# Attention's loads on GpSimd's queue, a bias made from its predecessor, and a fifth tile for the float16 probabilities

## The chip, the cores and the metric

The kernel runs on one core of a Trainium2 chip. The metric is the device time of one execution in microseconds (us), the median of several runs. The profile shows one further execution. Engines are named as in the profile: PE (TensorE matmuls), PEld (its weight loads), DVE (VectorE), ACT (ScalarE), POOL (GpSimd) and SP (SyncE); "SPq" is SP's queue, in which it issues DMAs in order.

## What is computed

A layer norm of x (1024 x 512) feeds two branches: grouped-query attention with 32 heads, 8 key/value heads and a linear position bias (ALiBi), and a feed-forward block with 4-bit weights. The result is x + attention * silu(ffn). The attention part of the reference, cut to what matters:

```python
q = _rmsnorm(q, q_norm_w); k = _rmsnorm(k, k_norm_w)
scores = jnp.einsum('bkgqd,bksd->bkgqs', qg, k) / math.sqrt(HD)
slopes = jnp.asarray(_alibi_slopes(H)).reshape(HKV, G)   # start * start**i, start = 2**(-1/4)
rel = pos[None, :] - pos[:, None]
bias = jnp.where(rel > 0, NEG_INF, slopes[:, :, None, None] * rel)
attn = jax.nn.softmax(scores + bias[None], axis=-1)
out = jnp.einsum('bkgqs,bksd->bkgqd', attn, v)
...
return out @ Wo.T
```

## The kernel before

The order of instructions on every engine is the order in which the program is written; there is no scheduler. The stages are: layer norm and the gate and up matmuls (to about 130 us), the down matmul (to about 215 us), twelve projections of keys, values and queries (to about 470 us), and the attention with its output projection (to the end). The last two projections share their time with the first eight steps of the attention.

Products keep near float32 precision: an operand is split into a high and a low part, and `mm3` (L108 to L110) adds three products. So keys (`kT`), values (`vT`), queries (`qT`) and probabilities are pairs of float16 tiles.

The projections write keys, values and queries to scratch in DRAM (`kd`, `vd`, `qd`). The attention loads them again: `load_keys` and `load_values` once a group of four heads (512 KB each), `load_queries` once a block of 256 query rows (512 KB), `load_wo` four times a group (256 KB each, output weights), and `gate_load` for the last four blocks (two of 512 KB each). All of these are issued by SP before the change.

A group has four blocks of 256 queries (qb = 0 to 3). Because of the causal mask, a block qb needs (qb + 1) x 256 keys at most. Groups 1 to 6 take the blocks in the order 2, 3, 0, 1; group 0 takes 3, 2, 1, 0; group 7 takes 2, 3, 1, 0. A block has four heads with two tiles of 128 queries each: eight steps, 256 steps in all. A tile's width is 128 to 1024 keys, so qb = 3 is called the wide block.

What happens to one tile, with the step at which it is issued (`step`):

- step n: `scores` on PE (tile s); PE waits where the two s tiles are still in use.
- step n + 1: `exponentials`. DVE adds the bias (`trel`, scaled for the head by `cs`) and finds the minimum (L799); ACT makes the exponential and its sum (L800), into `pf`.
- step n + 3: `split_hi`. ACT writes the high half of the scaled probabilities into a tile p16 (L810). The pool has `P16_BUFS` of these tiles, so it waits until the transpose of the tile so many places before has landed.
- step n + 4: `split_lo`. DVE writes the low half (L819), and SP issues the DMA that transposes the tile into `pT` (L820).
- step n + 9 (`AV_LAG`): `values` on PE multiplies pT with vT.

After that come `heads_hi` (ACT, L847), `heads_lo` (DVE, L853), `out_proj` (PE) and `accumulate` (DVE), one block later. `split_wo` splits the output weights: ACT writes woh (L769), POOL subtracts to get wol (L770). Raw weights `wor` have two buffers, which wol frees. `load_wo` stands 10 steps ahead of the projection it serves, `split_wo` 6 steps.

POOL also normalizes keys and queries in the projections (`newton` and `normalize`, tile f, L582 to L597), before DVE's `halves` (L608 to L610). That work for the last projection is spread over the attention, two tiles at a time. The bias of a group, `trel`, is made by POOL in `relative` (L775) from a fixed table of key minus query positions, `nrel` (L719 to L722), which is in SBUF throughout; `rc` is the reciprocal of the scale `cs`. `trel` has two buffers. A table or trel takes 4 KB of each partition, as does a p16 tile.

Of the kernel before, what the change touches and what calls it, by code (L numbers as in the profile page):

```python
# [10 lines left out]
F32 = mybir.dt.float32  # L11
# [5 lines left out]
ALU = mybir.AluOpType  # L17
# [4 lines left out]
P = 128  # L22
S = 1024
# [3 lines left out]
NH = 4  # L27
HD = 128
# [7 lines left out]
NQT = QB // P  # L36
# [22 lines left out]
GATE_SUMS = [27, 28, 30, 31]  # L59
GATE_STEP = 2  # L60
PF_BUFS = 5
P16_BUFS = 4

_START = 2 ** (-(2 ** (-(math.log2(H) - 3))))
SLOPES = np.array([_START * _START**i for i in range(H)], dtype=np.float32)
# [5 lines left out]
def attention_gated_by_ffn_kernel(ctx, tc, x, gu_w, gu_z, gu_s, dn_w, dn_z, dn_s, wq, wkv, wo, qnw, knw, out):  # L71
    nc = tc.nc
    ve, se, ge, te, sp = nc.vector, nc.scalar, nc.gpsimd, nc.tensor, nc.sync
# [46 lines left out]
    rc = const.tile([P, 1], F32, name="rc")  # L120
# [3 lines left out]
    kd = [dram.tile([P, 2, NT, 2 * HD], F16, name=f"kd{i}") for i in range(HKV // 2)]  # L124
    vd = [dram.tile([P, NT, 2 * HD], F16, name=f"vd{g}") for g in range(HKV)]
    qd = [dram.tile([NT, P, 2 * NH * HD], F16, name=f"qd{g}") for g in range(HKV)]
    ald = [dram.tile([1, 2 * HD], F32, name=f"ald{i}") for i in range(HKV // 2)]
    gd = dram.tile([NT, P, DM], F32, name="gd")
# [323 lines left out]
    def finish_step():  # L452

        for f in finishing.pop(clock[0], ()):
            f()
        clock[0] += 1
# [172 lines left out]
    def prepare(k, t):  # L629

        if k < len(projections):
            p = projections[k]
            if t == -1:
                p.squares()
            elif t == 1:
                p.norms()
            elif t == 2:
                p.scale()
            elif t == 6:
                p.factors()  # L640
            if 2 <= t < 2 + p.n:
                p.split_head(t - 2)
            elif p.kind == "kv" and 4 <= t < 6:
                p.split_values(t - 4)
# [31 lines left out]
    for it in range(NI):  # L676
        for tb in range(2):
# [14 lines left out]
            for i in range(4):  # L692
                c = slice(i * P, i * P + P)
# [23 lines left out]
    vp16 = left.enter_context(tc.tile_pool(name="values", bufs=1))  # L717
    fq = ctx.enter_context(tc.tile_pool(name="finish", bufs=2, side="right"))
    ap1 = ctx.enter_context(tc.tile_pool(name="attn1", bufs=2, side="right"))  # L719
    nrel = ap1.tile([P, S], F32, name="nrel", bufs=1)  # L720
    ge.iota(nrel, pattern=[[-1, S]], base=S - P, channel_multiplier=1, allow_small_or_imprecise_dtypes=True)
    ge.affine_select(nrel, nrel, pattern=[[-1, S]], compare_op=ALU.is_ge, fill=1e20, base=S - P, channel_multiplier=1)  # L722

    def queue_half(p, half):

        last = p is projections[-1]

        def due(steps, i, f):
            t = half * HT + i
            c = TILES - early + BS * (NB * (1 + t // 2) + FINISH_BLOCK) + 4 * (t % 2) if last else clock[0] + i  # L730
            finishing.setdefault(c + steps, []).append(f)

        due(0, 0, lambda: p.inverse(half))
        for i in range(3):
            due((i + 1) // 2, 0, lambda i=i: p.newton(half, i == 2))
        for i in range(HT):
            t = half * HT + i
            due(4, i, lambda t=t: p.halves(t))
            due(2, i, lambda t=t: p.normalize(t))
# [4 lines left out]
    kT, vT, qT, woh, wol = {}, {}, {}, {}, {}  # L744
    trel, pT, oT, wor = {}, {}, {}, {}

    def load_keys(g):
        kT[g] = ap1.tile([P, NT, 2, P], F16, tag="kT", name=f"kT{g}")
        sp.dma_start(kT[g].rearrange("p t a k -> p t (a k)"), kd[g // 2][:, g % 2])

    def load_values(g):
        vT[g] = ap1.tile([P, NT, 2, HD], F16, tag="vT", name=f"vT{g}")
        sp.dma_start(vT[g].rearrange("p t a d -> p t (a d)"), vd[g])

    def load_queries(g, qb):
        qT[g, qb] = ap1.tile([P, NQT, 2, NH, P], F16, tag="qT", name=f"qT{g}_{qb}")
        sp.dma_start(
            qT[g, qb].rearrange("p t a g q -> p t (a g q)"), qd[g][qb * NQT : (qb + 1) * NQT].rearrange("t p c -> p t c")
        )

    def load_wo(g, i):
        wor[g, i] = late[0].tile([P, DM], F32, tag="wor", name=f"wor{g}_{i}", bufs=2)
        sp.dma_start(wor[g, i], wo[(g * NH + i) * HD : (g * NH + i + 1) * HD, :])

    def split_wo(g, i):
        woh[g, i] = late[0].tile([P, DM], F32R, tag="woh", name=f"woh{g}_{i}", bufs=5)
# [4 lines left out]

    def relative(g):

        trel[g] = ap1.tile([P, S], F32, tag="trel", name=f"trel{g}")
        ge.tensor_scalar(trel[g], nrel, rc, float(SLOPES[g * NH + NH - 1]), ALU.mult, ALU.mult)  # L775

    s_ps, pf, rows16, p16, av_ps, op_ps = {}, {}, {}, {}, {}, {}

# [24 lines left out]
    def split_hi(u, qt):  # L803
# [4 lines left out]
        nk = pf[u, qt].shape[1]  # L808
        p16[u, qt] = ap1.tile([P, NT, 2, P], F16, tag="p16", name=f"p16_{u}_{qt}", bufs=P16_BUFS)[:, :nk]
        se.activation(p16[u, qt][:, :, 0, :], pf[u, qt], AF.Copy, scale=scale[:, qt : qt + 1])  # L810
# [56 lines left out]
    def gate_load(b):  # L867
        g, qb = blocks[b]
        gx = fq.tile([P, 2, NQT, DM], F32, tag="f", name=f"gx{qb}", bufs=3)
        t0 = qb * NQT  # L870
        sp.dma_start(gx[:, 0], gd[t0 : t0 + NQT].rearrange("t p c -> p t c"))
        sp.dma_start(gx[:, 1], x[t0 * P : (t0 + NQT) * P, :].rearrange("(t p) c -> p t c", p=P))
        gates[b] = gx

    def gate_partial(b, i):
# [30 lines left out]
    def step(n):  # L906
        nonlocal last_ps
        if n < nn:
            u, qt = order[n]
            g, qb, hh = units[u]  # L910
            b = u // NH
            if qt == 0 and hh == 1 and b + 1 < nb:
                load_queries(*blocks[b + 1])
            if qt == 0 and hh == 3 and g + 1 < HKV:
                if b % NB == KEYS_BLOCK:
                    relative(g + 1)
                    load_keys(g + 1)
                elif b % NB == VALUES_BLOCK:
                    load_values(g + 1)
            scores(u, qt)  # L920
# [34 lines left out]
        if r == 2 and b in GATE_LOADS:  # L955
            gate_load(nb - NB + GATE_LOADS.index(b))
        if b in GATE_SUMS and 0 <= r - GATE_STEP < NQT:
            gate_partial(nb - NB + GATE_SUMS.index(b), r - GATE_STEP)
        for lead, act in ((WO_SPLIT, split_wo), (WO_LOAD, load_wo)):
            w, r = divmod(m + lead, NB * BS)  # L960
            if 0 <= w < HKV and r in range(0, 2 * NH, 2):
                act(w, r // 2)

    last_ps = None
    early = 0
    for k, p in enumerate(projections):
        if k == len(projections) - 3:
            load_keys(0)
            load_values(0)
            load_queries(*blocks[0])  # L970
            relative(0)
        for t in range(NT):
            prepare(k + 1, t)
            if t == NT - 1:
                prepare(k + 2, -1)
            if k + 2 < len(projections) and t < KT:
                projections[k + 2].load(t)
            if t == HT:
                p.undo()
            p.tile(t)  # L980
            finish_step()
            if t % HT == HT - 1:
                queue_half(p, t // HT)
            if k >= len(projections) - 2 and t % 2 == 0:
                step(early)
                early += 1
# [46 lines left out]
```

## Time and profile before

| | |
|---|---|
| Time before | 1084.39 us median of 3 runs (1084.32 to 1085.37) |
| The profiled execution | 1091.69 us, span 1089.9 us |
| Mean granted PE clock | 0.984 |
| DMA issues of the attention's loads | 32 qT, 32 wor, 8 kT, 8 vT, 8 gx, all on SP |
| Transposes of p (pT<-p) | 256, median 4.0 us from issue to landing |

How to read it: the span is that of the profiled execution from its first to its last instruction. A stage's line lists for each engine the time in which it was busy and its instructions. A line of waits says who waited for whom, for how many us in total, how often, and the longest. In a timeline, a line has its start, its duration, engine, line of the program, operation, what is written from what, and in brackets the idle time before it with what ended it. An idle engine costs nothing unless the end of the program waits for it.

### The profile page before, as it was taken

What the parts mean: (1) busy time and instruction counts of PE and PEld (TensorE: products, weight loads), DVE (VectorE), ACT (ScalarE), POOL (GpSimd) and SP (SyncE); (2) the same over time, 40 slices, a digit from 0 to 9 for tenths busy, and PEclk for the clock granted to TensorE, in tenths of its full rate; (3) what the DMA queues carried; (4) which work ended last, traced back from release to release, by engine and by line L of the source; (5) the groups of instructions that cost most, each with busy time, mean ns of one, the idle gap of its engine ahead of it and who ended that gap; (6) DMA issues with size and microseconds to landing.
All of it is one profiled execution on the core that took longest, in us unless ns stands there. A gap on an engine that the chain in (4) does not pass through costs nothing.

```text
span 1089.9 us, 18604 instructions
## 1 busy us (share of the span) xinstructions
PE 1026.4 (94%) x5912; PEld 622.4 (57%) x5912; DVE 887.6 (81%) x1746; ACT 792.0 (73%) x2123; POOL 415.9 (38%) x551
## 2 busy tenths in 40 slices
PE   7899899999999898997999999999998999999986
PEld 4444378744444343445666666666665566666664
DVE  7888987448878888886898896998897878969974
ACT  5777633568786786787887796896886878868961
POOL 1588663137877878641105013023040030132222
PEclk8999999999999999998999999999999999999998
DMA  6123155237989999999989999998998999999993
GB/s 198 47 98 125 60 160 141 89 106 164 226 219 208 241 200 259 228 189 212 213 187 199 197 206 187 202 210 183 198 203 182 196 205 176 203 222 206 235 203 88
DMA packets 445888, 198.11 MB, mean 182 GB/s; under 512 B 394402, under 2 KB 403934, under 8 KB 445790
## 3 DMA queue, kind: packets, MB, share of 16 engines
q1 hardware_dynamic: 445790, 196.93, 82.6%
q8 instruction: 46, 0.75, 0.3%
q14 instruction: 52, 0.43, 0.2%
HBM read 71.03 MB, written 29.36 MB: 92 GB/s over the span
## 4 chain that ended last, share of the span: by engine, by line
PE 59%; DMA 13%; DVE 11%; ACT 8%; issue 5%; POOL 3%; SPq 1%; DVEq 0%; ACTq 0%; POOLq 0%
DMA pT<-p 12%; PE gu_ps L252 6%; PE av L108 4%; PE s L108 4%; PE s L109 4%; PE s L110 4%; PE av L109 4%; PE av L110 4%; PE ps_q L109 3%; PE ps_q L110 3%; PE op L110 3%; PE op L108 3%; PE ps_q L108 3%; PE op L109 3%; PE dn_ps L110 2%
## 5 line engine op out<-in xcount | busy, mean ns | idle before, releaser
L819 DVE SCALAR_TENSOR_TENSOR p<-pf,row,p 128x1024 f16<-128x1024 f32 (+7 forms) x256 | 216.6, 846 | 76.9 <-ACT p L810 74.8
L810 ACT ACTIVATE p<-pf,row 128x1024 f16<-128x1024 f32 (+7 forms) x256 | 197.0, 770 | 73.7 <-DMA pT<-p 70.2
L800 ACT ACTIVATE pf<-pf,row 128x1024 f32<-128x1024 f32 (+7 forms) x256 | 197.2, 770 | 38.5 <-DVE row L799 36.7
L770 POOL TENSOR_TENSOR wol<-wor,woh 128x512 fp32r<-128x512 f32 x32 | 59.8, 1870 | 429.5 <-ACT woh L769 373.6
L799 DVE CUSTOM_DVE_ANT_0 pf<-s,trel,cs 128x1024 f32<-128x1024 f32 (+7 forms) x256 | 207.5, 810 | 4.1 <-PE s L110 4.0
L108 PE MATMUL av<-pT,vT 128*128 128x256 f16 (+1 forms) x640 | 171.7, 268 | 25.2 <-DMA pT<-p 24.8
L109 PE MATMUL av<-pT,vT 128*128 128x256 f16 (+1 forms) x640 | 169.2, 264 | 0.0
L110 PE MATMUL av<-pT,vT 128*128 128x256 f16 (+1 forms) x640 | 169.0, 264 | 0.0
L108 PE MATMUL s<-kT,qT 128*128 128x512 f16 (+3 forms) x384 | 125.5, 327 | 6.6 <-DVE row L799 6.2
L109 PE MATMUL s<-kT,qT 128*128 128x512 f16 (+3 forms) x384 | 125.4, 327 | 0.0
L110 PE MATMUL s<-kT,qT 128*128 128x512 f16 (+3 forms) x384 | 123.8, 327 | 0.0
L108 PEld LDWEIGHTS <-vT 128*128 128x128 f16 x640 | 62.5, 98 | 106.9 <-issue 84.8
L108 PE MATMUL op<-woh,oh 128*128 128x512 f32 x248 | 121.7, 491 | 0.0
L109 PE MATMUL ps_q<-wl_q,xth 128*128 128x512 f16 x256 | 98.2, 383 | 6.7 <-DVE wl_q L528 6.7
L110 PE MATMUL op<-woh,ol 128*128 128x512 f32 x248 | 99.1, 400 | 0.0
L110 PE MATMUL ps_q<-wh_q,xtl 128*128 128x512 f16 x256 | 98.3, 384 | 0.0
L109 PE MATMUL op<-wol,oh 128*128 128x512 f32 x248 | 97.9, 395 | 0.4 <-POOL wol L770 0.4
L108 PE MATMUL ps_q<-wh_q,xth 128*128 128x512 f16 x256 | 98.2, 384 | 0.0
L847 ACT ACTIVATE oh<-av,rv 128x256 fp32r<-128x256 f32 x128 | 58.9, 460 | 24.9 <-PE av L110 24.4
L853 DVE SCALAR_TENSOR_TENSOR ol<-av,rv,oh 128x256 fp32r<-128x256 f32 x128 | 61.3, 479 | 13.6 <-ACT oh L847 13.5
L597 POOL TENSOR_TENSOR f_q<-f_q,inv_q 128x512 f32<-128x512 f32 x64 | 71.2, 1132 | 1.4
L109 PEld LDWEIGHTS <-vT 128*128 128x128 f16 x640 | 63.7, 100 | 12.2 <-issue 2.7
(179 smaller groups left out, 2315.1 us busy)
## 6 DMA issues: line engine op xcount, KB each, us to landing
qd<-tr_q SPq DMA_DIRECT2D x64, 256.0 KB, 3.6
qT<-qd SPq DMA_DIRECT2D x32, 512.0 KB, 4.4
wq<-in_wq SPq DMA_DIRECT2D x32, 256.0 KB, 3.9
wor<-in_wo SPq DMA_DIRECT2D x32, 256.0 KB, 3.7
gui<-in_gu_w SPq DMA_DIRECT2D x13, 512.0 KB, 3.6
wkv<-in_wkv SPq DMA_DIRECT2D x16, 256.0 KB, 3.8
vd<-v SPq DMA_DIRECT2D x8, 512.0 KB, 4.1
kd<-tr_kv SPq DMA_DIRECT2D x32, 128.0 KB, 2.5
```

What stands on the lines that cost most here:

```text
L108: te.matmul(ps, lhsT=lh, rhs=rh, start=first, stop=False)
L109: te.matmul(ps, lhsT=lh, rhs=rl, start=False, stop=False)
L110: te.matmul(ps, lhsT=ll, rhs=rh, start=False, stop=last)
L252: te.matmul(banks[j][:, k, :], lhsT=w[:, j, ws], rhs=x[:, j, k * 512 : k * 512 + 512], start=x is xth, stop=x is xtl)
L597: ge.tensor_tensor(f, f, ib, ALU.mult)
L770: ge.tensor_tensor(wol[g, i], raw, woh[g, i].bitcast(F32), ALU.subtract)
L799: ve.tensor_tensor_reduce(p, ps, trel[g][:, S - w :], cs[:, hh : hh + 1], 3e38, ALU.add, ALU.min, least[:, c])
L800: se.activation(p, p, AF.Exp, bias=least[:, c], scale=-1.0, accum_out=total[:, c])
L810: se.activation(p16[u, qt][:, :, 0, :], pf[u, qt], AF.Copy, scale=scale[:, qt : qt + 1])
L819: ve.scalar_tensor_tensor(lo, p, scale, hi, ALU.mult, ALU.subtract)
L847: se.activation(oh, av_ps[u], AF.Copy, scale=rv[:, g : g + 1])
L853: ve.scalar_tensor_tensor(ol, av_ps.pop(u), rv[:, g : g + 1], oh.bitcast(F32), ALU.mult, ALU.subtract)
```

## The change

Five loads (`load_keys`, `load_values`, `load_queries`, `load_wo`, `gate_load`) are issued by GpSimd (`ge`) and not by SP. The fixed table `nrel` goes: the first group's bias is built in its own tile, before the first projection, and each later group's is its predecessor's times the ratio of the two slopes, which is one half. The memory of the table goes to a fifth p16 tile.

```diff
-P16_BUFS = 4
+P16_BUFS = 5
...
-    nrel = ap1.tile([P, S], F32, name="nrel", bufs=1)
-    ge.iota(nrel, pattern=[[-1, S]], base=S - P, channel_multiplier=1, allow_small_or_imprecise_dtypes=True)
-    ge.affine_select(nrel, nrel, pattern=[[-1, S]], compare_op=ALU.is_ge, fill=1e20, base=S - P, channel_multiplier=1)
...
     def load_keys(g):
...
-        sp.dma_start(kT[g].rearrange("p t a k -> p t (a k)"), kd[g // 2][:, g % 2])
+        ge.dma_start(kT[g].rearrange("p t a k -> p t (a k)"), kd[g // 2][:, g % 2])
     def load_values(g):
...
-        sp.dma_start(vT[g].rearrange("p t a d -> p t (a d)"), vd[g])
+        ge.dma_start(vT[g].rearrange("p t a d -> p t (a d)"), vd[g])
     def load_queries(g, qb):
...
-        sp.dma_start(
+        ge.dma_start(
             qT[g, qb].rearrange("p t a g q -> p t (a g q)"), qd[g][qb * NQT : (qb + 1) * NQT].rearrange("t p c -> p t c")
         )
     def load_wo(g, i):
...
-        sp.dma_start(wor[g, i], wo[(g * NH + i) * HD : (g * NH + i + 1) * HD, :])
+        ge.dma_start(wor[g, i], wo[(g * NH + i) * HD : (g * NH + i + 1) * HD, :])
...
     def relative(g):
-        trel[g] = ap1.tile([P, S], F32, tag="trel", name=f"trel{g}")
-        ge.tensor_scalar(trel[g], nrel, rc, float(SLOPES[g * NH + NH - 1]), ALU.mult, ALU.mult)
+        rel = trel[g] = ap1.tile([P, S], F32, tag="trel", name=f"trel{g}")
+        if g == 0:
+            ge.iota(rel, pattern=[[-1, S]], base=S - P, channel_multiplier=1, allow_small_or_imprecise_dtypes=True)
+            ge.affine_select(rel, rel, pattern=[[-1, S]], compare_op=ALU.is_ge, fill=1e20, base=S - P, channel_multiplier=1)
+            ge.tensor_scalar(rel, rel, rc, float(SLOPES[NH - 1]), ALU.mult, ALU.mult)
+        else:
+            ge.tensor_scalar(rel, trel[g - 1], float(SLOPES[g * NH + NH - 1] / SLOPES[g * NH - 1]), None, ALU.mult)
...
     def gate_load(b):
...
-        sp.dma_start(gx[:, 0], gd[t0 : t0 + NQT].rearrange("t p c -> p t c"))
-        sp.dma_start(gx[:, 1], x[t0 * P : (t0 + NQT) * P, :].rearrange("(t p) c -> p t c", p=P))
+        ge.dma_start(gx[:, 0], gd[t0 : t0 + NQT].rearrange("t p c -> p t c"))
+        ge.dma_start(gx[:, 1], x[t0 * P : (t0 + NQT) * P, :].rearrange("(t p) c -> p t c", p=P))
...
     last_ps = None
+    relative(0)
     early = 0
     for k, p in enumerate(projections):
         if k == len(projections) - 3:
             load_keys(0)
             load_values(0)
             load_queries(*blocks[0])
-            relative(0)
```

## The prediction

> **What bounds the kernel now.** I read four views in this order: busy shares, TensorE's waits, the stages of the attention, and the DMA issues of SP's queue at one of the gaps.
>
> First the page's busy shares: TensorE is near full, so only its idle time can be won.
>
> ```profile
> PE 1026.4 (94%) x5912; PEld 622.4 (57%) x5912; DVE 887.6 (81%) x1746; ACT 792.0 (73%) x2123; POOL 415.9 (38%) x551
> ```
>
> Second, the stages of the attention from 500 to 1050 us (columns: stretch; its length; busy us and instructions of PE, PEld, DVE, ACT, POOL; granted clock; DMA share; GB/s).
>
> ```profile
> 500.00:600.00 100.00, 93.17 (x648) 64.41 (x647) 82.63 (x186) 79.02 (x181) 22.19 (x27) 0.97 1.02 201
> 600.00:700.00 100.00, 96.75 (x639) 65.05 (x637) 85.68 (x202) 79.73 (x186) 11.74 (x7) 0.98 0.99 198
> 700.00:800.00 100.00, 96.88 (x649) 65.00 (x649) 90.36 (x187) 82.52 (x176) 17.74 (x23) 1.00 0.97 202
> 800.00:900.00 100.00, 91.90 (x646) 63.81 (x645) 82.19 (x183) 75.84 (x174) 18.72 (x11) 1.00 0.99 193
> 900.00:1000.00 100.00, 97.76 (x651) 65.47 (x650) 84.15 (x191) 79.93 (x185) 20.02 (x13) 1.00 0.99 205
> 1000.00:1050.00 50.00, 46.72 (x317) 31.43 (x316) 42.41 (x81) 39.59 (x80) 13.50 (x8) 1.00 1.07 210
> ```
>
> 550.0 - 523.2 = 26.8 us in which TensorE does nothing. POOL has some 80% of its time free. The DMA share is a sum of packet times and exceeds 1, so it doesn't say that the engines are full.
>
> Third, who TensorE and ScalarE wait for from 460 us on:
>
> ```profile
> PE av L108 <- DMA pT<-p: 24.8, 20, 3.4
> PE s L108 <- DVE row L799: 6.2, 8, 1.8
> ACT p L810 <- DMA pT<-p: 70.2, 53, 4.9
> ```
>
> TensorE waits nearly only for the transposed probabilities pT. ScalarE waits for the same transposes, because they must let go of one of four p16 tiles (L810) before it can write the next.
>
> Fourth, one gap: SP's issues, then ScalarE's and TensorE's instruction at its end.
>
> ```profile
> 576.09 0.34 SPq L763 DMA_DIRECT2D wor<-in_wo  x1
> 576.48 4.62 SPq L820 DMA_TRANSPOSE pT<-p  x2
> 581.96 0.33 SPq L763 DMA_DIRECT2D wor<-in_wo  x1
> 582.41 8.57 SPq L820 DMA_TRANSPOSE pT<-p  x3
> 591.08 0.53 SPq L757 DMA_DIRECT2D qT<-qd  x1
> 591.71 8.57 SPq L820 DMA_TRANSPOSE pT<-p  x4
> 600.34 0.57 SPq L749 DMA_DIRECT2D kT<-kd  x1
> 601.01 3.77 SPq L820 DMA_TRANSPOSE pT<-p  x3
> ...
> 597.22 0.40 ACT L810 ACTIVATE p<-pf,row 128x128 f16<-128x128 f32 x1 [2.72 <-DMA pT<-p]
> ...
> 599.30 0.27 PE L108 MATMUL av<-pT,vT 128*128 128x256 f16 x1 [1.50 <-DMA pT<-p]
> ```
>
> From 582.4 us on, SP issues without a pause. I paired the 256 transposes in the trace with the 256 VectorE instructions (L819) that finish their tiles. SP's median issue time is 1.19 us for a tile of 128 columns, 1.56 us for 896 and 2.99 us for 1024. In block qb=2 of group 1 a transpose is through SP 1.4 us after its tile is ready; through block qb=3 this grows to 6.75 us, and block qb=0 starts with 6.0 us. Group 2 ends its wide block at 7.1 us, group 4 at 7.3 us. So SP is a late queue just where TensorE waits. Two loads also hold it up while they wait: after the first wide tile SP ends an issue at 575.11 us and then stands until 576.09 us, because the load of wor needs the buffer that POOL's wol frees ("SPq L763 waits for POOL wol": 12.9 us in 11 waits).
>
> **What the Trainium skill says.** "DMA: Bandwidth & Descriptors", section "Issuing engines are not separate DMA queues": DMAs of SP, ScalarE and GpSimd run on the same 16 engines and interleave, so another issuer saves only the sequencer's issue time. The trace agrees that issue time is the scarce thing here. Its section "SWDGE vs HWDGE vs iDMA" says that GpSimd's DMAs have their descriptors computed in software and kept in rings that the engines serve in turn with SP's. No DMA here is issued by GpSimd, so nothing shows its price. "SBUF — State Buffer", section "Who interferes with whom": a VectorE instruction with two SBUF inputs contends with GpSimd's reads, and a copy in a two-port mode blocks GpSimd while it runs, descriptor writing included. The trace fits the first: wol (L770) takes 1.27 us at its shortest and 1.87 us in the median. The second concerns few instructions of the attention, such as the casts q (L609).
>
> **The change part by part.**
>
> *Loads from SP to GpSimd.* Moved are 32 qT, 32 wor, 8 kT, 8 vT and 8 gx: 88 issues. By their durations (qT median 0.53, wor 0.61, kT and vT 0.57, gx 0.57 and 0.46) that is 32 x 0.53 + 32 x 0.61 + 16 x 0.57 + 4 x 0.57 + 4 x 0.46 = 50 us of SP's time, and the 12.9 us of waits for wol go too. In one group's wide block and after it (576 to 601 us) it is 2 wor, qT and kT, 0.34 + 0.33 + 0.53 + 0.57 = 1.8 us, and about 2 us of standing before the two wor. The transpose behind qT took 3.03 us where one of its width takes 1.56, so 1.5 us more. Together some 4 to 5 us of the 6.75 us backlog. What is left at the end of a wide block is about the 3 us that one transpose of 1024 columns needs.
>
> TensorE's gaps right behind the wide block of groups 1, 2, 4, 5, 6 and 7 (1.50, 2.30, 1.93, 1.44, 0.80, 3.29 us, at 599, 673, 822, 898, 969 and 1048 us) are each shorter than 4 us. I take all: -11.3 us. The other 23.4 - 11.3 = 12.1 us of waits for pT in the window lie in the first group (3.42 us at 510.6 us, behind four wor and a qT) and in blocks qb=0 and qb=1 (2.05, 1.59, 1.15). There the backlog is still draining, and the fifth tile helps; I take 80%, -9.7 us.
>
> *The fifth p16 tile.* L810 then waits for the transpose five tiles back, not four. ScalarE's 70.2 us in 53 waits are 1.3 us each, less than the 2 to 3 us between two landings in the wide block, so most go. Of itself this is worth nothing where SP is the late queue: ScalarE and VectorE would be early and the tiles would wait before SP. It counts with the other edit, and is in the 80%.
>
> *On POOL.* The instruction order of the new program shows PE, VectorE and ScalarE unchanged in sequence; POOL gets 88 DMA issues, SP loses them. POOL's cost of an issue is unknown: from below some 0.5 us, what SP needs; from above 2 us, an estimate, twice the page's about 1 us to the first byte on GpSimd's path ("Specifications"). I take 1.2 us: 88 x 1.2 = 106 us. Of them 81 lie in 500 to 1050 us, where POOL is busy 104 us of 550 and is covered. Behind a waiting load stand the next wol, the f_q of the last projection and y. The load of block b+1's queries waits for the last scores of block b-1, which TensorE finished two steps before the issue; the f_q of that step are needed two steps later, some 5 us. So I cost this at nothing. If that cover were gone, VectorE's cast q (L609) would wait for f_q, in 8 tiles.
>
> Where POOL is not free is 385 to 465 us (the last projections; it runs almost without a pause). There trel (1.16 us) goes and the first kT, vT and qT come, 3 x 1.2 us: +2.4 us on a chain that holds f_q and q. Between 0 and +5; I take +1.5.
>
> *The table.* The table's two POOL instructions (0.98 and 1.04 us at 219 us) stay, and trel of group 0 follows them, where POOL then idles 10.8 us: nothing. Later groups' single multiplication has 1.16 us to replace: nothing.
>
> *Transfers.* Bytes are the same. A qT had been ahead of the transposes behind it; now it shares with those already under way. Between -2 (no standing behind a load) and +20 (the rival below); I take +2.
>
> *Clock and end.* After the 3.42 us gap the clock shows 0.97 for that stretch; fewer gaps, -1. The end (1050 to 1090 us, 9.7 us idle) is a chain of its own: -1, of its 1.47 us wait for pT.
>
> Sum: -11.3 - 9.7 + 1.5 + 2 - 1 - 1 = -19.5 us against the profiled execution's 1091.7 us (span 1089.9). The gaps are one execution's, 7 us slower than the median of the timed runs; part of them may be smaller there, so I take 16.5 us from 1084.4: **1068 us**. What is late next is TensorE itself, then VectorE with 83 to 90% busy.
>
> **Rivals.**
>
> *The waits move (1077).* With SP free, VectorE (90% in 700 to 800 us) or the transposes' own landing, 4.0 us in the median and up to 7.4, holds pT. For it: 200 GB/s all along. Against it: before the wide blocks a transpose is through SP 1.4 us after its tile and no PE wait stands there. Only the standing and half the gaps go, 7 us.
>
> *Nothing shows (1084).* The gain is eaten by POOL's issues in the projections (+5) and slower landings.
>
> *Slower (1098).* Loads on their own ring share the engines with wide transposes. Per group some nine loads fall in blocks 1 to 3. One of 512 KB at the measured 200 GB/s is 2.6 us; if each takes half of that from the transposes beside it, 9 x 1.3 = 11.7 us per group. The 4.5 us relief absorbs part and the fifth tile 2.5; 4.7 us remain per group, of which TensorE, with AV_LAG as its cushion, sees some 2, 7 x 2 = +14 us. It decides once the median landing of pT rises from 4.0 us by more than the relief, to over some 7 us. Against it: sum of bytes and order of need are unchanged, and SP's ring loses what stood ahead.
>
> **How the numbers follow.** Forecast (gain 10 to 26 us) 0.55; waits move (gain 3 to 10) 0.17; nothing 0.08; slower 0.20. A measurement of this kernel can tell 0.2%, 2.2 us, from no change: faster 0.72, same 0.07, slower 0.21. The range 1058 to 1092 runs from a gain of all 26.8 us to the lower half of the slower case.
>
> **What would show it.** Right: "SPq L820" ends within 4 us of its tile in the block after a wide one, "ACT p <- DMA pT" falls from 70 to below 20 us, "PE av <- DMA pT" from 24.8 to below 8. Wrong: landings of pT well over 4.0 us, POOL instructions of over 2 us per load, f_q or woh waiting for POOL, or PE waits that come back as "s <- row". If ScalarE's wait goes and TensorE's stays, the backlog was not SP's.

## The result and the profile after

| | before | after |
|---|---|---|
| Median of the runs | 1084.88 us (1084.32 to 1086.26) | 1118.39 us (1117.77 to 1126.17) |
| Ratio after to before, 95% interval | | 1.0314 [1.0286, 1.0341] |
| Span of the profiled execution | 1089.9 us | 1116.5 us |
| Mean granted PE clock | 0.984 | 0.975 |

The kernel became 3.1% slower; 1068 us was predicted, and 1118 lies above the range. Medians here and below are of all executions, while ratios and their intervals leave out those that took over 1.5% longer than the fastest of the same kernel (one of e2's four, two of e9's four). The line numbers of the new program shift a little: L801 (row), L812 (ACT p), L821 (DVE p), L822 (the transpose of p), L767 (wol).

The page of after, busy shares:

```profile
PE 1028.8 (92%) x5912; PEld 624.8 (56%) x5912; DVE 898.1 (80%) x1746; ACT 793.3 (71%) x2123; POOL 482.1 (43%) x639
```

TensorE does the same 5912 matmuls. It is idle for 1116.5 - 1028.8 = 87.7 us; before it was 1089.9 - 1026.4 = 63.5. The 2.4 us that it was busy longer go with the lower clock. The waits of after from 460 us on, those of TensorE first (who waited for whom, total us, times, longest):

```profile
PE av L108 <- DMA pT<-p: 46.0, 20, 11.5
PE s L108 <- DVE row L801: 6.0, 6, 1.8
...
ACT p L812 <- DMA pT<-p: 41.1, 19, 10.8
...
POOL qT L754 <- PE s L110: 243.3, 20, 26.1
```

TensorE's wait for pT was 24.8 us before and is 46.0, in as many waits. Six of them (8.76, 2.80, 3.87, 4.57, 3.71 and 11.53 us) make up 35 us; the other fourteen are small. Before, none was longer than 3.4 us. The waits of up to 2.7 us sum to 18.1 us before and to 10.8 after: the short gaps have shrunk, and a few long ones have come. The stages in which the two longest lie (columns as before):

```profile
500.00:600.00 100.00, 86.37 (x582) 58.64 (x583) 72.83 (x160) 72.77 (x161) 21.89 (x21) 0.93 1.02 181
...
900.00:1000.00 100.00, 86.74 (x607) 60.92 (x607) 73.91 (x171) 71.20 (x168) 29.25 (x26) 0.94 1.01 197
```

In these two hundred microseconds TensorE was busy 93.17 and 97.76 us before. Now the longest wait in the timeline of after (start, duration, engine, line, operation, tiles, idle time before it):

```profile
979.73 0.73 POOL L873 DMA_DIRECT2D gx<-gd  x1
980.46 0.72 POOL L874 DMA_DIRECT2D gx<-in_x  x1
981.21 2.78 POOL L777 TENSOR_SCALAR trel<-trel 128x1024 f32<-128x1024 f32 x1
983.93 0.59 POOL L746 DMA_DIRECT2D kT<-kd  x1
986.09 0.71 POOL L754 DMA_DIRECT2D qT<-qd  x1 [1.56 <-PE s L110]
986.79 0.72 POOL L873 DMA_DIRECT2D gx<-gd  x1
987.50 0.70 POOL L874 DMA_DIRECT2D gx<-in_x  x1
988.19 0.57 POOL L750 DMA_DIRECT2D vT<-vd  x1
...
997.26 0.40 ACT L812 ACTIVATE p<-pf,row 128x128 f16<-128x128 f32 x1 [10.82 <-DMA pT<-p]
...
997.32 0.37 PE L108 MATMUL av<-pT,vT 128*128 128x256 f16 x1 [11.53 <-DMA pT<-p]
```

GpSimd hands in seven loads of 512 KB in nine microseconds. Before, SP had handed in the same seven between 967.9 and 986.8 us, with the transposes of the steps between them:

```profile
967.88 0.57 SPq L871 DMA_DIRECT2D gx<-gd  x1
968.51 0.46 SPq L872 DMA_DIRECT2D gx<-in_x  x1
969.08 2.49 SPq L820 DMA_TRANSPOSE pT<-p  x2
971.62 0.58 SPq L749 DMA_DIRECT2D kT<-kd  x1
972.31 5.12 SPq L820 DMA_TRANSPOSE pT<-p  x4
977.53 0.53 SPq L757 DMA_DIRECT2D qT<-qd  x1
978.16 2.99 SPq L820 DMA_TRANSPOSE pT<-p  x2
...
```

On GpSimd nothing keeps that distance. It stands where it has to wait itself, for the buffer of a qT ("POOL qT <- PE s", 243 us in all) or for woh before wol, and in between goes through several steps of the program at once. What these loads do to the transposes is in the trace: those issued by SP at 978.80, 983.45, 984.99 and 987.80 us land 18.4, 19.9, 20.8 and 18.3 us later. The second of them lands at 1003.34 us, behind three loads that were handed in after it (at 983.93, 986.09 and 986.79 us, landed at 999.82, 1001.17 and 1002.58). The landings of the transposes, from the view of the tile pT, first before and then after:

```profile
DMA to landing us min/median/max: 2.3/4.0/7.4
...
DMA to landing us min/median/max: 2.3/4.6/20.8
```

The trace shows a landing for 163 of the 256 transposes before and for 162 after; figures on landings are of these, here and in the other runs.

The median moved from 4.0 to 4.6 us only, the maximum from 7.4 to 20.8. And the wait costs twice, as the windows of after around it show (last columns: clock, DMA share, GB/s):

```profile
984.00:988.00 4.00, 1.78 (x15) 1.14 (x12) 1.52 (x7) 1.07 (x5) 2.44 (x4) 1.00 1.29 78
988.00:998.00 10.00, 0.68 (x4) 0.52 (x5) 0.30 (x1) 0.74 (x3) 0.77 (x2) 0.53 1.02 235
998.00:1002.00 4.00, 4.00 (x16) 2.45 (x15) 0.05 (x1) 0.16 (x2) 0.00 (x0) 0.50 1.21 292
```

From the wait's end to 1002 us TensorE works at a granted clock of 0.50. The first row shows 78 GB/s, though six of the seven loads and the four transposes have been or are being handed in; more of that below.

### The profile page after: what moved, and what is told of

Same layout as the page of the kernel before. It is cut to its first block, busy times and chain, and to the rows that moved or that the text cites. A ratio compares the mean times of both kernels' runs of the same rounds, so it can differ in the third digit from the quotient of the medians.

```text
span 1116.5 us, 18618 instructions
## 1 busy us (share of the span) xinstructions
PE 1028.8 (92%) x5912; PEld 624.8 (56%) x5912; DVE 898.1 (80%) x1746; ACT 793.3 (71%) x2123; POOL 482.1 (43%) x639
## 3 DMA queue, kind: packets, MB, share of 16 engines
q1 hardware_dynamic: 427998, 159.17, 70.2%
## 4 chain that ended last, share of the span: by engine, by line
PE 49%; DVE 17%; DMA 13%; ACT 8%; issue 7%; POOL 6%; SPq 0%; DVEq 0%; POOLq 0%; ACTq 0%
DMA pT<-p 12%; PE gu_ps L252 5%; PE av L108 4%; PE s L108 3%; PE s L109 3%; PE s L110 3%; PE av L110 3%; PE av L109 3%; PE op L108 3%; PE op L109 3%; PE op L110 3%; DVE pf L801 2%; DVE q L609 2%; DVE p L821 2%; PE dn_ps L110 2%
## 5 line engine op out<-in xcount | busy, mean ns | idle before, releaser
L821 DVE SCALAR_TENSOR_TENSOR p<-pf,row,p 128x1024 f16<-128x1024 f32 (+7 forms) x256 | 222.2, 868 | 55.7 <-ACT p L812 53.3
L812 ACT ACTIVATE p<-pf,row 128x1024 f16<-128x1024 f32 (+7 forms) x256 | 196.6, 768 | 45.1 <-DMA pT<-p 41.1
L801 DVE CUSTOM_DVE_ANT_0 pf<-s,trel,cs 128x1024 f32<-128x1024 f32 (+7 forms) x256 | 207.5, 810 | 24.1 <-PE s L110 23.1
L108 PEld LDWEIGHTS <-vT 128*128 128x128 f16 x640 | 62.9, 98 | 127.7 <-issue 97.3
L754 POOL DMA_DIRECT2D qT<-qd x32 | 23.4, 732 | 243.6 <-PE s L110 243.3
L767 POOL TENSOR_TENSOR wol<-wor,woh 128x512 fp32r<-128x512 f32 x32 | 58.5, 1828 | 159.8 <-ACT woh L766 159.8
```

The costliest lines, as they stand in the source:

```text
L108: te.matmul(ps, lhsT=lh, rhs=rh, start=first, stop=False)
L767: ge.tensor_tensor(wol[g, i], raw, woh[g, i].bitcast(F32), ALU.subtract)
L801: ve.tensor_tensor_reduce(p, ps, trel[g][:, S - w :], cs[:, hh : hh + 1], 3e38, ALU.add, ALU.min, least[:, c])
L821: ve.scalar_tensor_tensor(lo, p, scale, hi, ALU.mult, ALU.subtract)
```

## The experiments

The runs in one table, slowest last. "PE idle" is the span less TensorE's busy time; "PE for pT" is its wait for pT, "landing" the longest landing of a transpose of p, all from the profiled execution of each. Ratios are to the kernel before, run on the same chip beside each. The profiled execution need not be a median one: e3's is the fastest of its four, 8 us below its median, and that of before took 1091.69 us.

| run | loads on GpSimd | us | ratio, 95% interval | PE idle | PE for pT | landing |
|---|---|---|---|---|---|---|
| e7_wo_later | none | 1073.83 | 0.9906 [0.9884, 0.9928] | 55.6 | 16.6 | 7.5 |
| e4_wo_only | wor | 1078.07 | 0.9927 [0.9911, 0.9943] | 57.9 | 20.7 | 8.5 |
| e1_fifth_only | none | 1081.93 | 0.9967 [0.9954, 0.9980] | 61.5 | 24.4 | 7.4 |
| e10_before_wo9 | none | 1082.94 | 0.9980 [0.9969, 0.9991] | 60.2 | 18.0 | 7.3 |
| before | none | 1084.88 | 1 | 63.5 | 24.8 | 7.4 |
| e6_bunch_sp | none | 1094.90 | 1.0087 [1.0067, 1.0108] | 67.1 | 31.0 | 8.4 |
| e8_pace_dve | all, paced | 1100.82 | 1.0173 [1.0139, 1.0207] | 71.3 | 33.2 | 16.9 |
| e3_gate_sp | all but gx | 1101.64 | 1.0131 [1.0095, 1.0167] | 65.9 | 25.2 | 10.9 |
| e13_serial_late | all, one at a time | 1103.40 | 1.0167 [1.0125, 1.0208] | 71.4 | 18.1 | 8.8 |
| e11_big_act | none (ScalarE) | 1103.42 | 1.0201 [1.0161, 1.0242] | 77.9 | 37.0 | 12.3 |
| e5_serial | all, one at a time | 1109.14 | 1.0228 [1.0204, 1.0252] | 79.7 | 19.3 | 7.9 |
| e9_pace_landing | all, paced | 1114.72 | none (1097.65 to 1115.95) | 81.4 | 30.0 | 17.9 |
| e2_loads_only | all | 1118.06 | 1.0275 [1.0237, 1.0313] | 87.6 | 41.0 | 20.6 |
| after | all | 1118.39 | 1.0314 [1.0286, 1.0341] | 87.7 | 46.0 | 20.8 |
| e12_big_pool | all but wor | 1119.44 | 1.0319 [1.0301, 1.0337] | 85.7 | 43.9 | 13.2 |

Three theories are named in the expectations. F: the fifth tile or the halved bias does the harm. B: bunching, an issuer that isn't paced by the transposes hands in several loads at once. R: the second ring itself; at first in the form that two rings slow each other and cost DMA time in total, later, after the DMA-only kernel, in the form that a load on a second ring overtakes transposes already issued.

**One part alone (e1_fifth_only, e2_loads_only, e3_gate_sp).** The first is the changed kernel with its five loads back on SP:

```diff
-        ge.dma_start(kT[g].rearrange("p t a k -> p t (a k)"), kd[g // 2][:, g % 2])
+        sp.dma_start(kT[g].rearrange("p t a k -> p t (a k)"), kd[g // 2][:, g % 2])
...
```

> The changed kernel with all five loads back on SP: the fifth p16 tile and the halved bias alone. Theory R (two rings: GpSimd's loads run beside SP's transposes on the same 16 engines and slow them) and theory B (bunching: GpSimd isn't paced by SP's transposes, hands in several loads at once, and transposes wait behind the heap) both expect no loss: 1074 to 1086 us, ScalarE's waits for pT well below 70 us. Theory F (the fifth tile itself is the harm, more transposes in flight) expects about 1118 us.

The second is the kernel before with its five loads on GpSimd, the table and four p16 tiles kept.

> The kernel before with the five loads issued by GpSimd, four p16 tiles and the table kept. R and B expect the loss here: 1110 to 1130 us, with landings of pT of over 10 us. F expects the time before, 1080 to 1088 us.

The third is the changed kernel with the eight gx loads back on SP.

> The changed kernel with only the eight gx loads back on SP. In the changed kernel five of six loads that GpSimd issued within 9 us around 980 to 988 us end in an 11.5 us wait of TensorE, four of these loads are gx. B expects that wait gone and 1103 to 1111 us. R, for which a load costs wherever it falls (8 of 88), expects 1114 to 1119 us.

The fifth tile with the halved bias is a small gain, 0.3%; the loads alone cost what the whole change costs. F is out. Without the gx loads, which make the worst bunch, nearly half of the loss over e1 is gone (19.7 of 36.5 us are left), and the rest stays; 1101.6 us is a little below what B expected and far below R. The busy shares and the waits of e1:

```profile
PE 1018.6 (94%) x5912; PEld 619.4 (57%) x5912; DVE 891.0 (82%) x1746; ACT 794.4 (74%) x2123; POOL 426.1 (39%) x551
...
PE av L108 <- DMA pT<-p: 24.4, 23, 3.1
...
ACT p L812 <- DMA pT<-p: 31.9, 26, 3.2
```

The waits of e2:

```profile
PE av L108 <- DMA pT<-p: 41.0, 19, 12.6
...
ACT p L810 <- DMA pT<-p: 78.5, 42, 14.0
```

In e1 the fifth tile takes ScalarE's wait from 70.2 to 31.9 us, and TensorE's wait for pT doesn't move (24.8 to 24.4): ScalarE's wait was mostly slack. (How the 0.3% divides between the fifth tile and the halved bias was not tested.)

For e2 and the kernel before I paired each transpose with the VectorE instruction that finishes its tile, as in the prediction. From the tile to the end of SP's issue the mean falls from 3.38 to 2.48 us and the ninth decile from 6.48 to 4.05: the backlog on SP is relieved as forecast. From the tile to the landing the median falls too, from 5.60 to 4.94 us. But tiles that land over 11 us after they are ready go from 2 to 8, the latest from 12.1 to 23.4 us. The gain is spread over all tiles, where TensorE has slack; the loss sits in a few, where it has none.

**The DMAs alone (m1_rings).** This kernel leaves out the whole computation, and it was run once. It issues twelve transposes of 128 x 2048 on SP, with four loads of 512 KB between them on SP, at once on GpSimd, one by one on GpSimd, or on ScalarE:

```python
def mixed(engine):
    def issue():
        for i in range(NTR):
            if i % 3 == 1:
                engine.dma_start(ld[i // 3], gu_w[i // 3])
            transpose(i)
```

> Leaves the whole computation out: only DMAs, in phases that are separated by VectorE. Each of five phases has twelve transposes of 128 x 2048 float16 on SP: alone; with four loads of 512 KB issued by SP between them; with the four loads issued by GpSimd at once; with the four issued by GpSimd one by one, each after a transpose has landed; with the four issued by ScalarE at once. Then four loads alone on SP, and on GpSimd; all of it twice. R expects the phase with GpSimd's loads at least 4 us longer than the one with SP's, paced or not. B expects the phases equal within 1.5 us in their total, with single transposes landing more than 6 us later than alone.

From the first issue to the last landing it takes 37.4 and 37.9 us with the loads on SP, 34.4 and 33.7 with them on GpSimd at once, 38.95 and 37.6 one by one. R's forecast for the total (at least 4 us longer) failed. B's (equal within 1.5 us) holds for one by one, while the loads handed in at once are 3 to 4 us shorter. What differs is which transposes are late. Read from the trace (issued at, by, what, landed at, us later):

```
loads on SP
 47.81 SP     transpose  51.66  3.84
 49.18 SP     load       53.96  4.78
 49.98 SP     transpose  55.89  5.91
 53.88 SP     transpose  57.87  3.99
loads on GpSimd, one by one
127.39 SP     transpose 134.51  7.12
127.51 GpSimd load      132.78  5.27
136.20 SP     transpose 143.47  7.28
136.86 GpSimd load      143.26  6.40
four loads on GpSimd at once
 87.58 GpSimd load       96.08  8.50   (the fourth)
 88.05 SP     transpose  97.99  9.94
 95.61 SP     transpose  99.87  4.25
```

On SP's ring the transpose ahead of a load lands on time (3.7 to 4.8 us), and the one behind it comes late (5.9 to 7.0 us in all eight cases). With a load on another ring both come late. In eight cases a transpose was issued 0.07 to 0.91 us before the load; SP's own ring has no such close pair, since SP issues a load 1.4 to 2.5 us behind a transpose. The transpose lands after 5.7 to 9.5 us, and the next one after 6.6 to 9.0. In five of the eight the load lands first, by up to 1.8 us, so it overtakes; in three the transpose lands first, by up to 0.7 us. The loads are late too, after 5.1 to 8.8 us, where the first load of those on GpSimd with nothing beside it lands after 3.6. So a load on a second ring shares the engines also with the transposes ahead of it, and these lose most.

With four loads handed in, the first transpose, which is issued behind them, lands only after the last load, with ScalarE's ring as with GpSimd's (9.0 and 7.9 us). No phase has four loads and then a transpose all on SP, so this says nothing about the rings. The Trainium skill has a statement that fits: "DMA: Bandwidth & Descriptors", section "Queues, rings and completion order", says that each engine takes turns between rings and drains a whole packet of several descriptors from one before it switches. In the packets' records one of a load is 4096 bytes and takes 159 ns undisturbed, one of a transpose 256 bytes and 18 ns. If both packets hold equally many descriptors, the load gets 159 of 159 + 18 parts of the time, an estimate from that page. No run shows the turns themselves, and loads that come 1.5 to 5 us late don't bear out a share as large as that.

**Is it bunching (e5_serial, e6_bunch_sp), and is wor part of it (e4_wo_only)?** In e5 GpSimd hands in a load only when its last one has landed:

```diff
+            ge.tensor_copy(seen, prev)
...
+        one_at_a_time(kT[g][:, 0, 0, 0:1])
         ge.dma_start(kT[g].rearrange("p t a k -> p t (a k)"), kd[g // 2][:, g % 2])
...
```

> The changed kernel, but GpSimd hands in a load only when its load before has landed (it first copies one element of the tile loaded last). The loads stay on the second ring, with at most one under way. Theory B: the two long TensorE waits (8.8 and 11.5 us) go, the largest landing of pT falls from 20.8 to under 11 us, time 1080 to 1090 us. Theory R: still each load overtakes transposes; TensorE's waits for pT stay over 35 us and the time over 1105 us. GpSimd itself waits some 5 us per load, 81 loads from 500 us on; if f_q or wol come late by that, up to +6 in both.

TensorE's waits in e5:

```profile
PE av L108 <- DMA pT<-p: 19.3, 15, 2.7
PE s L108 <- DVE row L818: 9.9, 5, 5.1
PE ps_kv L108 <- DVE v L555: 7.5, 1, 7.5
...
PE s L108 <- DMA qT<-qd: 6.2, 2, 5.3
```

Both numbers of B for pT came (longest landing 7.9 us, no long wait, even less waiting than before), and its time didn't; R's time came, without its waits. New waits took the place: GpSimd stood 6.33 us for kT and 5.25 us for vT in the projections, VectorE then waited 10.69 us for f_q and TensorE 7.5 us for VectorE; later qT came late. So a run with that standing taken out: e13_serial_late applies the rule only from step 8 on.

> As the run with one load at a time on GpSimd (1109 us), but the rule holds only from step 8 on (about 470 us), so that GpSimd no longer stands for kT and vT in the projections (6.3 and 5.3 us there, behind which VectorE waited 10.7 us for f_q and TensorE 7.5 us). If GpSimd's own standing is what kept that run slow, while one load at a time does protect pT: 8 to 13 us less, 1096 to 1101 us, TensorE's wait for pT stays near 19 us. If the second ring costs even with one load under way: 1105 to 1111 us, TensorE's waits for pT over 30 us.

```profile
PE av L108 <- DMA pT<-p: 18.1, 13, 4.2
PE s L108 <- DVE row L819: 10.0, 6, 4.5
PE s L108 <- DMA qT<-qd: 8.0, 1, 8.0
```

The wait for v is gone and the time is 1103.4 us, 5.7 less, short of the 8 to 13 expected (its runs spread from 1096.67 to 1110.74). Against e1 TensorE is idle 9.9 us more: 8.0 for a qT that stood in GpSimd's row, 5.0 more for row, 3.1 more for wol, 0.9 more at the end, less 6.3 for pT and 0.8 elsewhere. Another 8.7 us of its longer span are the same matmuls at a granted clock of 0.979 in place of 0.992. One load at a time protects pT, and GpSimd then becomes too late for its other work.

In e6 all loads are on SP, but keys, values and queries of a group come at one step, and before the last group four gx loads with them:

```diff
             if qt == 0 and hh == 1 and b + 1 < nb:
+                if b == nb - NB - 1:
+                    gate_load(nb - NB)
+                    gate_load(nb - NB + 1)
+                if g + 1 < HKV and b % NB == VALUES_BLOCK:
+                    load_keys(g + 1)
+                    load_values(g + 1)
                 load_queries(*blocks[b + 1])
```

> All loads on SP (1082 us), but bunched: keys, values and queries of the next group at one step, and before the last group four gate loads together with these three (3.5 MB, 17.5 us at 200 GB/s). Theory B (bunching is harmful on any ring): transposes behind the bunch land up to 18 us later, TensorE waits some 8 to 12 us once and 1 to 3 us in each of six groups: 1095 to 1110 us. Theory R (the second ring is the harm): within 4 us of 1082, because transposes ahead of the loads aren't overtaken.

1094.9 us is 13 above e1, at B's lower edge, and R's forecast failed. A bunch costs on one ring too. There it doesn't show as B had it, in late landings and a wait of 8 to 12 us: no landing takes over 8.4 us and no wait over 5.5, since the transposes stand in SP's queue behind the bunch. Of the 15.1 us by which the profiled span is longer than e1's, 5.6 are idle time of TensorE and 9.5 the same matmuls at a lower granted clock (0.981).

In e4 only wor is on GpSimd (e1 with that one line).

> The changed kernel with keys, values, queries and gate loads back on SP; only the 32 wor loads (256 KB each, evenly spread, two steps apart) stay on GpSimd. Reference: with all loads on SP it took 1082 us. Theory B (the harm is that GpSimd, not paced by the transposes, hands in several loads at once): wor never comes with a second large load, so within 4 us of 1082, and below it by up to 3 us because SP no longer stands for wol. Theory R (any load on a second ring costs, because it overtakes transposes that were handed in before it): by bytes wor is 8 of 36 MB, so 8/36 of the loss of 36 us = +8, 1090 us.

1078.07 us, 3.9 below e1: small, evenly spread loads on the second ring do no harm that exceeds the gain of SP not standing for wol. R's estimate by bytes (1090) is out.

**Pace without one load at a time (e8_pace_dve, e9_pace_landing).** Before each load (once for a pair of gx) GpSimd copies one element that a given step has made, the row minimum of two steps before or the pT of five steps before. Loads of one step are still handed in together:

```diff
+        n = now[0]
+        if at(n - 2):
+            u, qt = at(n - 2)
...
+            ge.tensor_copy(seen, rows16[u][0][:, qt : qt + 1])
```

> The changed kernel, but before a load GpSimd copies one element of the minimum that VectorE found two steps before, so that loads are handed in at their own step and not in a bunch when GpSimd has run ahead. They still go on the second ring, beside transposes that are under way. Theory B (bunching by an engine that isn't paced): no more than two large loads at once, the largest landing of pT falls from 20.8 to under 11 us, TensorE's long waits for pT go; 1080 to 1092 us. Theory R (a load on the second ring overtakes the transposes handed in before it, wherever it falls): 1100 us or more.

> The changed kernel, but before a load GpSimd copies one element of pT that the transpose of five steps before has written, so a load is handed in only when that transpose has landed, about where SP stood with it before the change. Theory B: as with VectorE's pace, 1080 to 1092 us. Theory R: the loads now overtake fewer transposes, so better than with VectorE's pace by 5 us or more. GpSimd is held by up to two steps (some 5 us); if f_q comes late by that, VectorE's wait for it rises from 23 us and the time by up to +8.

Both missed B. Paced by VectorE the kernel takes 1100.8 us, half-way back, just inside R's forecast. Paced by the landings its four runs took 1097.65, 1113.68, 1115.76 and 1115.95 us. That is too wide apart for a ratio, but none is better than e8's median by the 5 us of R's forecast. What remained in e8 is one place above all, its timeline:

```profile
494.01 0.71 POOL L770 DMA_DIRECT2D qT<-qd  x1
494.72 0.20 POOL L753 COPY seen<-row 128x1 f32<-128x1 f32 x1
494.84 0.58 POOL L777 DMA_DIRECT2D wor<-in_wo  x1
...
510.66 0.39 PE L108 MATMUL av<-pT,vT 128*128 128x256 f16 x1 [12.06 <-DMA pT<-p]
```

A qT and a wor of the same step, 768 KB, which at the 200 GB/s of the stages would need some 4 us, take until 508.2 and 510.3 us, and so does the transpose beside them (issued 493.67, landed 510.61). The windows of e8 say that the engines did not move much meanwhile:

```profile
499.00:502.00 3.00, 0.00 (x0) 0.00 (x0) 2.81 (x6) 1.77 (x5) 0.00 (x0) 0.64 1.14 110
502.00:505.00 3.00, 0.00 (x0) 0.00 (x0) 0.15 (x2) 0.00 (x0) 0.00 (x0) 0.50 1.22 99
505.00:508.00 3.00, 0.00 (x0) 0.00 (x0) 0.00 (x0) 0.00 (x0) 0.00 (x0) 0.50 1.19 90
```

In e9 it is a pair of gx loads (1 MB, issued 1028.0 and 1028.7, landed 1042.2 and 1045.6) with 72 GB/s from 1032 to 1036. There TensorE works on, and its wait of 8.7 us comes later, at 1041 us. The DMA share is over 1 all the while, so it says that packets took long and not that bytes moved.

**GpSimd, or any second ring (e11_big_act, e12_big_pool)?** Both have wor on SP. The 56 large loads are ScalarE's in the first, whose steps follow the scores and which can't run ahead; they are GpSimd's in the second. The edit is one word per load (`ge` to `sp` for wor in both, `ge` to `se` for the 56 in the first).

> The changed kernel with wor on SP and keys, values, queries and gate loads (56 loads, 512 KB each) issued by ScalarE: a second ring again, but one whose descriptors hardware makes, and an issuer that passes its steps with the scores and so can't run ahead. If any second ring is the harm: 1095 to 1110 us, landings of pT of over 11 us, stretches of some microseconds in which the engines move under 110 GB/s. If it is GpSimd's own way of handing in (its ring, or its running ahead): 1080 to 1088 us, no such stretch; ScalarE's 56 issues of some 0.5 us are 28 us on an engine with 27% free, up to +4.

> The same 56 loads on GpSimd, wor on SP: the counterpart of both the ScalarE run and of the run with wor alone on GpSimd (1078 us). If the harm comes with the large loads on GpSimd's ring, it is as slow as with all loads there, 1105 to 1118 us; if wor's share is a real part of it, 1090 to 1105 us.

TensorE's wait in e11:

```profile
PE av L108 <- DMA pT<-p: 37.0, 17, 6.9
```

And in e12:

```profile
PE av L108 <- DMA pT<-p: 43.9, 24, 5.1
```

With ScalarE as the issuer 1103.4 us: a second ring costs 21 us over e1 without GpSimd, as the first reading of its expectation had it, with a longest landing of 12.3 us. Two things are in these 21 us that weren't tested apart. ScalarE's own 56 issues take 22.3 us of its time. And bunches are not gone: before its longest wait (6.9 us, to 978.4) ScalarE hands in three loads of 512 KB at 964.3, 968.3 and 968.7 us. GpSimd adds 16 (1119.4, just above the first reading of its expectation). e12 is as slow as after without a wait for pT over 5.1 us: it has 24 waits for pT in place of 20, and its matmuls take 1032.8 us in place of 1028.8.

**One step later (e7_wo_later, e10_before_wo9).** SP's standing before wor can be had without another ring:

```diff
-WO_LOAD = 10
+WO_LOAD = 9
```

> All loads on SP (1082 us), wor loaded one step later (WO_LOAD 9 for 10), so that wol has freed the buffer by the time SP comes to the load. SP's standing for wol (14.7 us in 11 waits) falls below 5 us. If SP's standing is what makes pT late behind the wide blocks, as my prediction had it, 2 to 5 us less: 1077 to 1080 us. If the transposes' own rate in the wide block is the limit, no difference: 1081 to 1083 us.

> The kernel before with nothing but WO_LOAD 9 for 10. With the fifth tile the same step was worth 8 us (1082 to 1074). If SP's standing before wor is the cost by itself: 1077 to 1079 us. If ScalarE's wait for a p16 tile must go first: within 2 us of the kernel before, 1083 to 1086.

SP's wait for wol in e7, which was 14.7 us in e1:

```profile
SPq L760 <- POOL wol L767: 1.1, 1, 1.1
```

e7 takes 1073.83 us, 0.94% less than the kernel before, the best of all and better than the 1077 to 1080 expected. With the four tiles of the kernel before (e10) the same edit takes 0.2% only, so ScalarE's wait had to go first, as its second reading had it. The fifth tile with the halved bias takes 0.33% by itself; both together take more than the sum.

## Why the prediction was wrong

- *What bounds the kernel.* Right: TensorE's waits for pT, and SP's backlog as one source. e7 shows it: 13.6 us less standing of SP, 8 us less time.
- *Loads from SP to GpSimd* (-11.3) and *the fifth tile* (in the -9.7). Half right. SP's backlog fell (e2: ninth decile 6.48 to 4.05 us), and the waits for pT of up to 2.7 us fell from 18.1 to 10.8 us. That the fifth tile is worth little by itself, since the tiles then stand before SP, came true: in e1 the mean from the tile to the end of SP's issue is 3.97 us, 3.38 before. So the sign "If ScalarE's wait goes and TensorE's stays, the backlog was not SP's" would have misled: e1 shows it, and SP's backlog is longer there than before.
- *On POOL.* 0.55 to 0.79 us an issue, where I took 1.2. In the projections (+1.5) the size was right: from 385 to 465 us TensorE is busy 75.7 us, 76.75 before. The cover held in after: "DVE q <- POOL f_q" is 26.6 us after 22.4. What its loss costs, e5 showed: 7.5 us of TensorE at one place.
- *Transfers* (+2). This is the step that failed. I wrote that a moved qT "shares with those already under way" and took +2 us, with no working for the 2. The runs showed that the transposes under way come off far worse: they land up to 20.8 us after their issue (7.4 before), some behind loads that were handed in later. The loads cost the difference of after and e1, 1118.4 - 1081.9 = 36 us, and that is net of what SP's relief gained. So the term was some +36 us at least.
- The step behind it: I cost the new queue at little but issue time. SP's order was also a pace. On GpSimd the loads wait for a buffer and then come together.
- *Slower (1098)* was the rival that came true, in kind. Two things in it were off. Its price, half of a load's time by bytes and +14 us in all, was less than half of the true one. And its point of decision, "median landing of pT rises ... to over some 7 us", looked at the wrong number: the median went to 4.6 us. In after the long waits come from the latest landings (up to 20.8 us); e12 loses as much with landings up to 13.2 us and more, shorter waits. "Sum of bytes and order of need are unchanged" was no argument against it; the order of service changed.
- *Clock* (-1). The sign was wrong. Against e1 the profiled span of after is 36.4 us longer: 26.2 of idle TensorE (21.6 of it for pT) and 10.2 of the same matmuls at a clock of 0.975 in place of 0.992. A part of this kind is in every slow run, and no run separates it from the waits.

How the 36 us divide is argued and not shown. By medians, a bunch on SP's own ring costs 13 (e6 - e1), a second ring with another issuer 19 to 21 (e8, e11 - e1), and GpSimd in place of ScalarE 16 (e12 - e11); by the ratios it is 13, 22 to 25 and 13. 13 to 16 and 19 to 21 sum to about the whole loss. But e8 and e11 still have loads that are handed in together, and no set of runs has bunching and the second ring switched on and off in all four combinations with the same loads. Nor is it tested whether GpSimd's 16 us come from its running ahead or from its ring. What is shown: the loads on GpSimd are the loss (e1, e2), the small ones alone cause none (e4), and with one load at a time the waits for pT fall below e1's (e5, e13).

Still open is why the rate falls for some microseconds while loads and transposes are under way on two rings, to 100 GB/s over nine microseconds of e8. One cause that the prediction mentions, VectorE copies that keep GpSimd from writing descriptors, is out for that place: by the windows of e8, VectorE is busy for 0.15 us from 502 to 508 us. And a short fall doesn't need two rings. The windows of before have one too, with three transposes of SP under way (issued at 899.7, 901.2 and 902.5 us, landed at 905.2 to 905.9); TensorE works on through it:

```profile
903.00:906.00 3.00, 3.00 (x20) 1.94 (x19) 1.42 (x5) 1.36 (x5) 0.00 (x0) 1.00 1.09 51
```

## What to carry to other kernels

A queue is also an order and a pace: before a load is moved to another engine's queue, ask what it will now overtake and what will hand it in early. Judge transfers on the critical path by the latest landings and by the waits that end on them, not by the median or the bytes. If an engine's DMA queue stands for a buffer, try first to issue that load a step later; here this gave 0.9% with the fifth tile, and the second ring took 3%.

## What was not expected of the hardware

- A load on another ring slows the transposes issued before it, and can overtake them: a transpose issued 0.12 us ahead of the load landed 7.1 us after its issue and 1.7 us behind the load, and the transpose at the start of the same phase after 3.9. On one ring the transpose ahead landed after 3.8 us.
- The fifth tile with the halved bias lowered ScalarE's wait by 38 us and TensorE's by 0.4, for 0.3% of time; with SP relieved as well the two were worth more than their sum.
- After a wait of 11.5 us TensorE ran at a granted clock of 0.50 for nearly 5 us more (997.3 to 1002 us in after). It isn't a matter of long waits alone: in before a wait of 3.4 us, to 510.6 us, is followed by a clock of 0.50 from 510.7 to 516.5 us.
